# Token layers of a scan and attention hybrid: four images one behind the other in place of layer by layer, two of them beside the last outputs

## The chip, the cores and the metric

The kernel runs on one core of a Trainium2 chip. The metric is the device time in microseconds of one launch on that core. Before the change it is 10757.76 us, the median of 8 runs (10748.81 to 10774.99).

## The reference

The input is x, four images of 64 by 64 positions with 96 channels. Four layers follow, each added onto x:

```
x = x + conv_ref(group_norm(x), ...)          # layers 0 and 1: selective scan in four directions
t = tokens(x)                                 # (4, 4096, 96)
t = t + attn_ref(layer_norm(t), ...)          # layer 2, attention without softmax
t = t + ffn_ref(layer_norm(t), ...)           # layer 2, feed-forward in quantised floats
t = t + attn_ref(layer_norm(t), ...)          # layer 3
t = t + ffn_ref(layer_norm(t), ...)           # layer 3
```

The attention has no softmax: `y = (q @ k.T * D**-0.5) @ v` by head, so that k.T @ v can be formed first, from the Gram matrix of the normalised tokens. The feed-forward (96 to 384 to 96, relu between) rounds inputs and weights to a float of 5 exponent and 2 mantissa bits, and sums to half precision. All sums of an image's attention and all its norms need only that image: no layer mixes images. In a layer of selective scan, the output of an image is `layernorm(y) * silu(z)` times a matrix, added onto x.

## The kernel before, in words

The kernel is written for a scheduler that takes the instructions in the order of the program, places them on each engine's queue by priority of that order as soon as it reckons them ready, and gives out the buffers of a pool in the order in which the program asks for them. Tiles of one tag share that tag's buffers. Inside the scans (`scan_pair`, line 331) the class `InOrder` holds each engine to the program's order; their instructions are all recorded at line 71.

Four units of work come first: two scan layers, each in two pairs of images (lines 864 to 869). Before each unit `between_scans` (line 104) runs the outputs of the unit before (`scan_outputs`, line 247) beside the inputs of the next (`scan_inputs`, line 123), as two generators that are stepped in turn. After the fourth unit the outputs of images 2 and 3 of layer 1 run alone (line 869). `scan_outputs` goes over 16 groups of 256 positions. In each it loads zt, ys and xr, normalises ys (DVE statistics at 281, a power on POOL at 81, ACT at 289), transposes six blocks into the tile pt (296), scales them to gt on ACT (299), multiplies by zt on DVE (306), multiplies by the output matrix into po (310, 311), adds xr (313) and stores both images (316).

Then come the token layers. Each image is one tile tok of 128 partitions by 32 tokens by 96 channels, loaded at line 876. `attention` (718) runs for all four images, then `ffn` (774) for all four, then both again for layer 3 (lines 877 to 879). Each of the four calls opens pools of its own for weights, for work tiles and for PSUM, and closes them at its end; so their memory passes from one call to the next.

- `token_norm` (680): 32 statistics on DVE (684), six small steps on DVE, one power on POOL (81) for all 32 tokens of a partition, the shift (699), and 32 scalings into tn, 24 on ACT (705) and 8 on POOL (703).
- `attention`: 32 products on PE into gram (754), eight groups of four transposes into tnps with a copy to tnt on ACT (714, 715), four small products one after the other (739) with DVE between them, then eight groups of four products into ops (769) and a sum onto tok on DVE (771).
- `ffn`: eight transposed groups as above into xq (715), then eight chunks of 512 tokens. A chunk has three products into hps (809), each with a copy to h16 on ACT (811), bias and relu into hb16 on DVE (813) and a cast to hq on POOL (814); then twelve products into ops (818), a copy to o16 on ACT (822), a sum on DVE with the bias (824) and one onto tok (826). In layer 3 tok is then stored (828).

tn, tnt, xq, h16, hb16, hq, o16 and ob16 have two buffers each. In PSUM, hps of the feed-forward has three and tnps, ops, gram and small have two.

Of the kernel before, what the change touches and what calls it, by code (L numbers as in the profile page):

```python
# [16 lines left out]
F32 = mybir.dt.float32  # L17
BF16 = mybir.dt.bfloat16
F16 = mybir.dt.float16
E5M2 = mybir.dt.float8e5  # L20
AF = mybir.ActivationFunctionType
ALU = mybir.AluOpType
# [81 lines left out]
def between_scans(tc, cst, ident, half, u, before, after):  # L104


    with ExitStack() as stage:
        if before is None:
            for _ in scan_inputs(tc, stage, cst, ident, half, u, *after):
                pass  # L110
        elif after is None:
            for _ in scan_outputs(tc, stage, ident, half, *before):
                pass
        else:
            ins = scan_inputs(tc, stage, cst, ident, half, u, *after)
            for _ in scan_outputs(tc, stage, ident, half, *before):
                for _ in range(2):
                    next(ins, None)
            for _ in ins:
                pass  # L120
# [126 lines left out]
def scan_outputs(tc, stage, ident, half, layer, pr):  # L247
# [4 lines left out]
    pp = stage.enter_context(tc.tile_pool(name="c_ps", bufs=1, space=PSUM))  # L252
# [3 lines left out]
    for g in range(NT // 2):  # L256
# [36 lines left out]
        pt = pp.tile([128, 3, 2, 128], F32, name="pt")  # L293
        for j, first in enumerate((0, 256, 128)):
            for t in range(2):
                nc.tensor.transpose(pt[:, j, t], ys[:, t, first : first + 128], ident)
        gt = p2.tile([128, 3, 2, 128], F32, name="gt")
        for s, js in ((0, slice(0, 2)), (1, slice(2, 3))):
            nc.scalar.activation(
                gt[:, js],  # L300
                pt[:, js],
                AF.Identity,
                bias=par[:, s, P_NB : P_NB + 1],
                scale=par[:, s, P_NW : P_NW + 1],
            )
        nc.vector.tensor_tensor(gt, gt, zt.rearrange("p j (t q) -> p j t q", q=128), ALU.mult)
        po = pp.tile([128, 2, 2, C], F32, name="po")
# [372 lines left out]
def token_norm(nc, pool, half, t, tn):  # L680

    stats = pool.tile([128, NT, 6], F32, name="tstats")
    for j in range(NT):
        nc.vector.bn_stats(stats[:, j], t[:, j])  # L684

# [13 lines left out]
    nc.vector.scalar_tensor_tensor(shift, mean2, -0.5, rs, ALU.mult, ALU.mult)  # L699
    for j in range(NT):  # L700
        scale, bias = rs[:, j : j + 1], shift[:, j : j + 1]
        if j % 4 == 3:
            nc.gpsimd.tensor_scalar(tn[:, j, :C], t[:, j], scale, bias, ALU.mult, ALU.add)  # L703
        else:
            nc.scalar.activation(tn[:, j, :C], t[:, j], AF.Identity, bias=bias, scale=scale)  # L705


def turn_tokens(nc, pp, ident, tn, out):

    n = tn.shape[2]  # L710
    for g in range(NT // 4):
        ps = pp.tile([n, 512], F32, name="tnps", tag="tp")
        for j in range(4):
            nc.tensor.transpose(ps[:, 128 * j : 128 * j + 128], tn[:, 4 * g + j], ident)  # L714
        nc.scalar.activation(out[:, 512 * g : 512 * g + 512], ps, AF.Copy, saturate=False)


def attention(tc, cst, ident, half, tok, w):


    nc = tc.nc
    with ExitStack() as stage:
        p1 = stage.enter_context(tc.tile_pool(name="t1", bufs=1))
        p2 = stage.enter_context(tc.tile_pool(name="t2", bufs=2))
        pp = stage.enter_context(tc.tile_pool(name="t_ps", bufs=2, space=PSUM))

        wkv = p1.tile([C + 1, 2 * C], F32, name="wkv")
        nc.sync.dma_start(out=wkv, in_=w["wkv"])
        wq = p1.tile([C, C + 1], F32, name="wq")
        nc.sync.dma_start(out=wq, in_=w["wq"])  # L730
        wff = p1.tile([C, C], F32, name="wff")
        nc.sync.dma_start(out=wff, in_=w["Wff"])
        bff = p1.tile([C + 1, C], F32, name="bff")
        nc.sync.dma_start(out=bff, in_=w["bff"])

        def product(a, b, name):

            ps = pp.tile([a.shape[1], b.shape[1]], F32, name=name, tag="small")
            nc.tensor.matmul(ps, a, b, start=True, stop=True)
            return ps  # L740

        def kept(ps, name):
            to = p2.tile(list(ps.shape), F32, name=name)
            nc.vector.tensor_copy(to, ps)
            return to

        for b in range(NB):
            t = tok[b]
            tn = p2.tile([128, NT, C + 1], F32, name="tn")
            nc.gpsimd.memset(tn[:, :, C : C + 1], 1.0)  # L750
            token_norm(nc, p2, half, t, tn)
            gram = pp.tile([C + 1, C + 1], F32, name="gram")
            for j in range(NT):
                nc.tensor.matmul(gram, tn[:, j], tn[:, j], start=(j == 0), stop=(j == NT - 1))  # L754
            tnt = p2.tile([C + 1, L], F32, name="tnt")
            turn_tokens(nc, pp, ident, tn, tnt)
            gk = kept(product(kept(gram, "gram"), wkv[:, :C], "gkps"), "gk")
            vk = product(wkv[:, C:], gk, "vkps")

            heads = p2.tile([C, C], F32, name="heads")  # L760
            nc.vector.tensor_tensor(heads, cst["heads"], vk, ALU.mult)
            rest = kept(product(heads, wff, "hps"), "rest")
            whole = p2.tile([C + 1, C], F32, name="whole")
            nc.vector.tensor_tensor(whole, bff, product(wq, rest, "wps"), ALU.add)
            for g in range(NT // 4):
                po = pp.tile([128, 4, C], F32, name="ops", tag="o")
                for j in range(4):
                    at = 512 * g + 128 * j
                    nc.tensor.matmul(po[:, j], tnt[:, at : at + 128], whole, start=True, stop=True)  # L769
                tg = t[:, 4 * g : 4 * g + 4]  # L770
                nc.vector.tensor_tensor(tg, tg, po, ALU.add)


def ffn(tc, ident, half, tok, w, out=None):

    nc = tc.nc
    NH = HID // 128
    with ExitStack() as stage:
        p1 = stage.enter_context(tc.tile_pool(name="f1", bufs=1))
        p2 = stage.enter_context(tc.tile_pool(name="f2", bufs=2))  # L780
        pp = stage.enter_context(tc.tile_pool(name="f_ps", bufs=2, space=PSUM))

        def quantised(shape, src, name, back=False):
            raw = p1.tile(shape, F32, name=name)
            nc.sync.dma_start(out=raw, in_=src)
            q = p1.tile(shape, E5M2, name=name + "q")
            nc.vector.tensor_copy(q, raw, saturate=False)
            if back:
                nc.vector.tensor_copy(raw, q)
                return raw  # L790
            return q

        w1 = quantised([C, HID], w["W1"], "w1")
        w2 = quantised([128, NH, C], w["W2"].rearrange("(k p) c -> p k c", p=128), "w2")
        b1 = quantised([128, NH], w["b1"], "b1", back=True)
# [197 lines left out]
```

## Time and profile before

| what | us |
|---|---|
| median of 8 runs | 10757.76 |
| the profiled execution | 10772.43 |
| its span | 10770.6 |
| last outputs (10079 to 10204) | 125 |
| attention of layer 2 (10204 to 10335) | 131 |
| feed-forward of layer 2 (10335 to 10470) | 135 |
| attention of layer 3 (10470 to 10600) | 130 |
| feed-forward of layer 3 (10600 to 10771) | 171 |
| busy over the span: DVE, POOL, ACT, PE | 9622.8, 9028.6, 8755.0, 8109.2 |

The limits of the stages are those at which the work of one layer gives way to that of the next; neighbours overlap by a few us. PE is the time of matmuls, PEld that of weight loads, which lie beside them. DVE is VectorE, ACT ScalarE, POOL GpSimd, SP the queue from which transfers are issued. An instruction on SP counts only as issue, its transfer takes place later.

### The profile page before, as it was taken

The page shows a single profiled execution, that of the slowest core. Times are in us where ns is not written, and L with a number is a line of the kernel's source. Part 1 is how long each engine was busy: PE and PEld are TensorE (multiplying, and loading weights), DVE is VectorE, ACT ScalarE, POOL GpSimd, SP SyncE. Part 2 cuts the span into 40 slices and gives each one's busy share as a digit, 9 for nine tenths or more (in the row PEclk, how much of TensorE's full clock was granted, in tenths as well). Part 3 has the DMA queues.
Part 4 walks back from the last instruction along what each step waited for, and adds up shares of the span by engine and source line. Part 5 has one row for each costly group of instructions (what it writes and reads, how often), then busy time and mean ns, then how long its engine had stood idle before and what let it go on. Part 6 is the DMA issues. An engine that isn't in the chain of part 4 may idle for free. (4 is left out here: it accounts for less than half of the span.)

```text
span 10770.6 us, 143139 instructions
## 1 busy us (share of the span) xinstructions
PE 8109.2 (75%) x48032; PEld 6010.1 (56%) x48032; DVE 9622.8 (89%) x6898; ACT 8755.0 (81%) x18679; POOL 9028.6 (84%) x5306
## 2 busy tenths in 40 slices
PE   7777777777777777776877777777777777777666
PEld 4555555554555555555555555555455555555544
DVE  7999999997899999998899999999699999999655
ACT  6988888885898888886688888888588888888556
POOL 3999999992899999996599999999299999999444
PEclk9888898888888898998888888889888989898766
DMA  3677777775677777777577777777477777777600
GB/s 123 208 211 215 217 224 219 213 217 144 193 211 214 218 219 221 217 220 196 153 209 215 214 219 219 218 218 213 139 208 210 218 215 222 215 220 219 177 3 26
DMA packets 960473, 2114.17 MB, mean 196 GB/s; under 512 B 413526, under 2 KB 704664, under 8 KB 762008
## 3 DMA queue, kind: packets, MB, share of 16 engines
q1 hardware_dynamic: 959736, 2105.01, 68.0%
q8 instruction: 381, 6.24, 0.3%
q14 instruction: 356, 2.92, 0.1%
HBM read 1943.27 MB, written 161.48 MB: 195 GB/s over the span
## 5 line engine op out<-in xcount | busy, mean ns | idle before, releaser
L71 POOL TENSOR_TENSOR h<-h,cb 128x1024 f32<-128x1024 f32 x3072 | 7193.6, 2365 | 232.3 <-issue 57.9
L71 DVE TENSOR_TENSOR_SCAN h<-da,last,bp 128x1024 f32<-128x1024 f32 x2064 | 4736.7, 2335 | 144.8 <-PE bp L71 22.6
L71 ACT ACTIVATE x<-dut,bt 128x128 f32<-128x128 f32 x12288 | 3495.2, 370 | 1.3 <-PE bp L71 1.0
L71 PE MATMUL yp<-ident,h 128*128 128x128 f32 x24576 | 3352.9, 296 | 10.2 <-POOL h L71 10.2
L71 PEld LDWEIGHTS yp<-ident,h 128*128 128x128 f32 x24576 | 3179.4, 156 | 126.1 <-issue 75.1
L71 ACT ACTIVATE da<-delta,amat 128x1024 f32<-128x1024 f32 x2752 | 3060.7, 1138 | 96.9 <-DVE h L71 95.9
L71 PE MATMUL bp<-ident,x 128*128 128x128 f32 x10240 | 1674.5, 315 | 1293.4 <-DVE h L71 953.3
L71 PEld LDWEIGHTS bp<-ident,x 128*128 128x128 f32 x10240 | 1355.9, 162 | 1857.3 <-ACT x L71 1024.5
L71 DVE TENSOR_TENSOR bp<-du,bp 128x1024 f32<-128x1024 f32 x1472 | 1779.9, 1213 | 301.9 <-PE bp L71 300.1
L71 DVE TENSOR_TENSOR_SCAN h<-da,bp 128x1024 f32<-128x1024 f32 x688 | 1537.5, 2274 | 48.0 <-ACT da L71 8.5
L71 PE MATMUL bp<-bparts,sel 96*128 96x512 bf16 x2944 | 924.0, 399 | 756.9 <-DVE h L71 741.8
L71 PEld LDWEIGHTS <-sel 96*128 96x128 bf16 x2944 | 227.0, 100 | 1552.3 <-DVE h L71 1040.9
L71 ACT ACTIVATE bp<-delta,amat 128x1024 f32<-128x1024 f32 x320 | 358.4, 1120 | 525.7 <-DVE h L71 524.0
L71 POOL TENSOR_TENSOR dbu<-du,bb 128x1024 f32<-128x1024 f32 x320 | 755.1, 2360 | 0.0
L81 POOL TENSOR_TENSOR ln_rs<-ln_ve,half 128x4 f32<-128x4 f32 x64 | 83.9, 1311 | 593.4 <-DVE ln_ve L79 492.2
L71 DVE TENSOR_TENSOR_SCAN h<-bp,last,dbu 128x1024 f32<-128x1024 f32 x240 | 558.9, 2329 | 16.3 <-POOL dbu L71 15.1
L71 PE MATMUL xps<-u,wx 128*76 128x512 f32 x768 | 559.9, 818 | 5.7 <-ACT cdt L71 2.9
L71 POOL TENSOR_TENSOR du<-delta,u 128x1024 f32<-128x1024 f32 x192 | 506.6, 2638 | 21.7 <-ACT delta L71 21.7
L71 POOL COPY last<-h 128x2 f32<-128x2 f32 x1152 | 216.1, 188 | 341.4 <-DVE h L71 340.5
L71 ACT ACT_TABLE_LOAD x384 | 492.7, 1283 | 6.8
L71 PE MATMUL dps<-cdt,wdt 12*128 12x512 f32 x768 | 448.0, 665 | 0.0
L71 ACT COPY dut<-dups 128x512 f32<-128x512 f32 x384 | 220.7, 575 | 257.7 <-PE dups L71 257.7
(132 smaller groups left out, 6384.0 us busy)
## 6 DMA issues: line engine op xcount, KB each, us to landing
cb<-crow SPq DMA_DIRECT2D x1024, 1024.0 KB
cb<-crow SPq DMA_DIRECT2D x1024, 512.0 KB
bb<-crow SPq DMA_DIRECT2D x384, 256.0 KB
bb<-crow SPq DMA_DIRECT2D x128, 512.0 KB
y<-ysum SPq DMA_DIRECT2D x192, 256.0 KB
kept<-y SPq DMA_DIRECT2D x160, 256.0 KB
y<-ysum SPq DMA_DIRECT2D x64, 512.0 KB
zt<-zg SPq DMA_DIRECT2D x64, 384.0 KB
```

The costliest lines, as they stand in the source:

```text
L71: return self.tc.keep_in_program_order(getattr(self.engine, op)(*args, **kwargs))
L81: nc.gpsimd.tensor_tensor(rs, ve, half, ALU.pow)
```

## The change

The token layers become one function, `token_layers`, in which every image is a generator that runs attention and feed-forward of layer 2 and then of layer 3, and yields between small pieces: every 8 statistics, after the scale, every 8 scalings, every group of transposes, every group of attention sums, and twice in each chunk of the feed-forward. A layer pair of one image is some 51 such pieces. The loop steps the last scan outputs by one group and every image that has begun by one piece in each turn. Image b begins no earlier than turn 13 b; images 0 and 1 may begin while the outputs of images 2 and 3 still run, images 2 and 3 only once they are done, when their tok is loaded.

For that, all weights of both layer pairs are loaded at the start, and all token work shares one set of pools. The scan's large tiles are in pools that close before the token layers open theirs. tn has three buffers. hps goes from three PSUM buffers to two, gram and small from two to one. The last outputs use the PSUM tags of the token layers ("mm" for the transposes, "o" for the sums). In all four output stages the tile pt, six blocks in one buffer of two banks, becomes three blocks for each half of the tokens, in two buffers of one bank, and the two scalings on ACT become four.

```diff
-        pt = pp.tile([128, 3, 2, 128], F32, name="pt")
-        for j, first in enumerate((0, 256, 128)):
-            for t in range(2):
-                nc.tensor.transpose(pt[:, j, t], ys[:, t, first : first + 128], ident)
         gt = p2.tile([128, 3, 2, 128], F32, name="gt")
-        for s, js in ((0, slice(0, 2)), (1, slice(2, 3))):
-            nc.scalar.activation(
-                gt[:, js],
-                pt[:, js],
...
+        for t in range(2):
+            pt = pp.tile([128, 3, 128], F32, name="pt", tag=turned)
+            for j, first in enumerate((0, 256, 128)):
+                nc.tensor.transpose(pt[:, j], ys[:, t, first : first + 128], ident)
+            for s, js in ((0, slice(0, 2)), (1, slice(2, 3))):
+                nc.scalar.activation(
+                    gt[:, js, t],
+                    pt[:, js],
...
-        po = pp.tile([128, 2, 2, C], F32, name="po")
+        po = pp.tile([128, 2, 2, C], F32, name="po", tag=summed, bufs=1 if summed == "po" else None)
...
-    for n in (2, 3):
-        attention(tc, cst, ident, half, tok, {k: a[f"l{n}_{k}"] for k in ("wq", "wkv", "Wff", "bff")})
-        ffn(tc, ident, half, tok, {k: a[f"l{n}_{k}"] for k in ("W1", "b1", "W2", "b2")}, a["out"] if n == 3 else None)
+def token_layers(tc, cst, ident, half, x, outputs, a):
...
+        load(0)
+        load(1)
+        wa = [weights(attention_weights, n, ("wq", "wkv", "Wff", "bff")) for n in (2, 3)]
+        wf = [weights(ffn_weights, n, ("W1", "b1", "W2", "b2")) for n in (2, 3)]
...
+        def image(b):
+            for n in range(2):
+                yield from attend(n, b)
+                yield from feed(n, b)
+
+        outs = scan_outputs(tc, stage, ident, half, *outputs, pp, "mm", "o")
+        images = [image(b) for b in range(NB)]
+        begun, going, turns = 0, [], 0
+        while outs is not None or going or begun < NB:
+            if outs is not None and next(outs, outs) is outs:
+                outs = None
+                load(2)
+                load(3)
+            if begun < NB and turns >= 13 * begun and (begun < 2 or outs is None):
+                going.append(images[begun])
+                begun += 1
+            going = [one for one in going if next(one, going) is not going]
+            turns += 1
```

In the changed kernel `token_norm`, `attention` and `ffn` are generators over one image, with the same instructions in the same order within an image; `turn_tokens` makes one group of four transposes a call, so that in `attention` the eight groups stand between the gram products.

## The prediction

> **What bounds the kernel now.** I read first the page's row of busy tenths over the span (in its last slices DVE falls from 9 to 6 and 5, ACT to 5 and 6, POOL to 4), then busy time by stretch, then the groups of instructions by shape, the waits, and the order of time where they pointed. The change leaves the scans as they are, so the tail counts: the last outputs (10079 to 10204), attention of layer 2, feed-forward of layer 2, attention and feed-forward of layer 3. Columns: stretch, length, then busy us of PE, PEld, DVE, ACT, POOL, granted clock, DMA share, GB/s.
>
> ```profile
> 10079.00:10204.00 125.00, 74.15 (x352) 62.18 (x352) 52.42 (x192) 49.39 (x96) 16.10 (x16) 0.66 0.60 166
> 10204.00:10335.00 131.00, 85.75 (x680) 82.61 (x680) 60.79 (x297) 59.83 (x151) 46.37 (x50) 0.75 0.10 39
> 10335.00:10470.00 135.00, 86.03 (x532) 49.47 (x532) 83.30 (x210) 100.03 (x218) 84.82 (x110) 0.63 0.00 1
> 10470.00:10600.00 130.00, 93.11 (x741) 86.06 (x740) 67.82 (x280) 60.13 (x145) 45.55 (x54) 0.76 0.02 5
> 10600.00:10771.00 171.00, 99.18 (x608) 54.99 (x608) 103.66 (x276) 116.38 (x256) 106.56 (x132) 0.61 0.09 38
> 10204.00:10771.00 567.00, 364.08 (x2560) 273.13 (x2560) 315.57 (x1060) 336.36 (x768) 283.30 (x344) 0.68 0.06 22
> ```
>
> No engine is full. In the last row four engines do 364 + 316 + 336 + 283 = 1299 us of work in 567: 2.29 engines at a time. Attention has its own shape (PE ahead), feed-forward another (ACT ahead), and they stand one after the other for all four images. The waits of the tail say why:
>
> ```profile
> POOL tn_rs L81 <- DVE tn_ve L79: 158.4, 14, 47.9
> ...
> DVE tshift L699 <- POOL tn_rs L81: 90.7, 16, 8.7
> ...
> ACT tn L705 <- DVE tshift L699: 81.7, 8, 21.2
> ```
>
> ACT stands 82 us before norms whose scale isn't there. At the first one (order of time) statistics start at 10204.6, the 5.4 us power on POOL follows, and ACT starts at 10217.2. What can be reached is seen inside a feed-forward, chunk after chunk:
>
> ```profile
> 10646.79 0.54 DVE L826 TENSOR_TENSOR tok<-tok,ob 128x384 f32<-128x384 f32 x1
> 10647.26 0.96 DVE L813 TENSOR_SCALAR hb<-h,b 128x512 f16<-128x512 f16 x2
> 10648.31 0.78 DVE L824 TENSOR_TENSOR ob<-o,b 128x384 f16<-128x384 f16 x1
> 10649.01 0.70 DVE L813 TENSOR_SCALAR hb<-h,b 128x512 f16<-128x512 f16 x1
> 10649.63 0.54 DVE L826 TENSOR_TENSOR tok<-tok,ob 128x384 f32<-128x384 f32 x1
> ```
>
> A chunk takes 10649.63 - 10646.79 = 2.84 us with DVE nearly full. In 10640 to 10656 the engines were busy 12.24 + 14.71 + 11.72 + 12.60 = 51.3 us in 16: 3.2 at a time, the best that the tail shows. Without norms 32 chunks would take 91 us; the two feed-forwards took 135 and 171.
>
> **The Trainium skill.** "Perfetto Trace Analysis", Optimization Strategy: where the busiest engine changes from regime to regime, interleaving the regimes may help as well as work inside each. The first table agrees that it changes. "TensorE: Matmul & The Clock Gate", What's actually happening: idleness halves TensorE's clock, sustained work releases it. The trace agrees: sixteen products of L769 took 3.41 us at 10529.6 and 1.79 at 10552.6. "GPSIMD Engine Reference", Specifications: POOL shares its SBUF interface with VectorE. The cast of L814 is spread from 602 to 957 ns (median 804), which fits and doesn't prove it. "PSUM — Partial Sum Buffer", Specifications: eight banks of 2 KiB a partition; no run here shows it, and I use it for the count below.
>
> **The change part by part.**
>
> *Start.* The loads of images 0 and 1 and 16 weight loads now stand on SP ahead of the loads of the last outputs. In the built order (the order in which the changed program queues its instructions on each engine) the image loads come before the last store of the scan's sum (10074.6), the weights after it. The image loads wait for memory of the scan's inputs, whose last readers on PE and DVE end at about 10062 to 10069; behind them on SP stands that store alone, which is not ready before 10074.6, so this wait costs nothing. If their 3 MB were still moving when the outputs' first loads come, those loads would land later; that is in the upper bound. SP issues of such weights took 0.28 to 0.94 us at 10055 to 10058; 16 x 0.5 = 8 us. They push wo, zt and ys, which all outputs wait for, by about 8 us. On DVE the 64 statistics of images 0 and 1 stand ahead of the first ystats: 64 x 0.17 us (33 took 5.52) = 11 us, mostly inside that delay. I take 10 us, bounds 4 and 16.
>
> *Outputs.* 125 us for 16 groups is 7.8 us a group: po on PE (3.6 us), rest of pt (1.3), gt on ACT (1.2), gt by zt on DVE (1.0). pt is split by token half into two PSUM banks (1536 B each, before 3072 B in one two-bank buffer). By shape gt took 778 + 557 = 1335 ns. Two halves of 128x256 (557) and 128x128 (estimate 447, by the slope of the two) are 2008: ACT gains 0.67 x 16 = 11 us in each output stage. In the three stages between scans ACT is busy 109 of 227 us against PE 181, so that is hidden; the second pt buffer could give a little. I take 0, bounds -8 and +8 each, in sum -15 to +15 as they needn't add up. In the last outputs the split lets gt of one half start early, and norms of images put ACT work between; I keep 125 us, bounds 105 and 145.
>
> *What runs beside the outputs.* By the built order only normalisation, gram, transposes and the small products of images 0 and 1: their attention sums share tag "o" with the sixteen po and come after the last. Moved, a quarter or an eighth of each group: ACT tn 145.0/8 + tnt 35.7/4 = 27; DVE stats 91.0/8, small steps 2.7, products 2.5 = 17; POOL power 86.8/8 and tn 52.5/8 = 18; PE gram 63.4/4, transposes 40.3/4, products 3 = 29. Together 90 us of engine work, so half an attention of two images and not more.
>
> *After the outputs.* 1299 - 90 = 1209 us of work remain, with attention of one image beside feed-forward of another (built order: "0: xq, 2: tnt, 0: h ..." on ACT). Layer barriers, weight waits and three of four ramps go. Norms of one image should lie beside chunks of another. At 2.9 engines at a time that is 417 us. I chose 2.9 between 2.29 (today's mean) and 3.2 (best stretch), nearer the best, because norm gaps get a cover but queues in fixed order and two buffers each of h16, hb16, hq stay. Check on ACT: 336 - 27 = 309 us; at the start it must wait for the sums, statistics and power (some 25 us), at the end image 3 is nearly alone (10): 309/(417 - 35) = 81%, against 74% in the first feed-forward. hps goes from three buffers to two, gram and small from two to one (2+2+2+1+1 = 8 banks): PE needs 0.5 us for hps, ACT 0.59, so two suffice; 0, bound +5. The last store (6 us) stays.
>
> *Sum.* Outputs start at 10079 + 10, end at 10214, the rest ends at 10631: 10771 - 10631 = 140 us gone of the profiled execution, which took 10772.43 (span 10770.6 and 1.8 around it). That run is 14.7 us over the median, 10757.8; the saving taken off the median gives 10618.
>
> **Rivals.**
> 1. *Queues mesh better (10564).* At 3.2 engines throughout the rest takes 1209/3.2 = 378 us, and the outputs are 15 us shorter as PE warms up: 140 + 39 + 15 = 194 us saved. For it: no engine passes 364 us of 567. Against: DVE is already 92% full in that stretch.
> 2. *Fixed order eats it (10705).* At 2.4 the rest takes 504 us, 53 saved: DVE's queue mixes statistics of one image between hb and ob of another, and each wait holds all behind it. The wait ACT tn <- DVE tshift would stay near 80 us.
> 3. *Slower (10788).* One chunk in flight at a time: tag slots and DVE's order join the images. Unpipelined a chunk is transposes 0.9, xq 0.6, hps 0.5, h 0.6, hb 0.6, three hq 2.3, ops 1.4, o 0.5, ob 0.7, tok 0.6 = 8.7 us; 64 of them 557, with 35 for the ramps 592, ending at 10806: 35 us slower, less 5 of chunks that do overlap. It decides from 8.1 us a chunk ((557 - 35)/64). Against: 2.84 today.
> 4. *It doesn't do what it says:* half true above, since the attention sums can't pass the outputs; counted in the sum.
>
> **How the numbers follow.** Forecast (95 to 178 us saved) 0.48; rival 1 (more) 0.25; rival 2 (22 to 95) 0.21; rival 3 0.04; within 0.2% 0.02, a bound that is about what a measurement of this kernel can tell from no change. The likeliest is 10618. From 10550 (rival 1 and between-stage gain 15) to 10695 (2.45 at a time, 63 saved) I leave out some 7% below and 13% above. Faster 0.48 + 0.25 + 0.21 = 0.94.
>
> **What would show it.** First ystats about 10095; last xo about 10214; no gram work of images 2 and 3 before it; four engines' work in the rest near 1209 us in about 417; ACT tn <- tshift well under 82 us; the 64 casts o about (417 - 35)/64 = 6 us apart on the mean. Wrong if the outputs pass 150 us, if granted clock stays at 0.6 while PE becomes the last wait, or if ACT's 25 us start gap recurs at each layer.

## The result and the profile after

The changed kernel takes 10719.68 us, the median of 10 runs (10708.31 to 10730.28), the kernel before beside it 10762.04 (28 runs): a ratio of 0.9961, 95% interval 0.9953 to 0.9969. It is faster by 42 us, where 140 were predicted, and 10719.68 lies outside the range of 10550 to 10695. The profiled execution has a span of 10717.9 us, against 10770.6 before, so the two traces differ by 53 us, 10 more than the medians do.

The start of the tail wanders from profile to profile with the scans ahead of it, which no kernel here changes: over all twenty profiles the scan's last copy to ysum on ACT starts between 10060.5 and 10108.3 us. I therefore measure the tail from that copy (10073.6 before, 10075.5 after). The tail was 697.0 us and is 642.4: 55 us less. Busy time by stretch of the changed kernel (columns as in the prediction; the count of instructions is in brackets): up to the first ystats, to the last xo, to the first copy h of a feed-forward chunk, to the end.

```profile
10075.50:10107.70 32.20, 4.21 (x26) 4.21 (x27) 12.31 (x78) 5.73 (x15) 9.46 (x12) 0.52 0.72 215
10107.70:10224.50 116.80, 84.00 (x539) 73.61 (x537) 55.21 (x214) 77.04 (x180) 25.32 (x25) 0.79 0.50 136
10224.50:10277.80 53.30, 34.99 (x178) 32.59 (x178) 28.09 (x145) 18.37 (x50) 17.42 (x19) 0.56 0.17 64
10277.80:10717.90 440.10, 290.33 (x2175) 216.99 (x2174) 257.07 (x816) 286.84 (x654) 244.09 (x304) 0.79 0.04 15
```

The first ystats comes 32.2 us after the scan's last copy (11.3 before); the outputs then take 116.8 us (116.1 before). What follows the last xo is 53.3 + 440.1 = 493.4 us (569.6 before). In it PE, DVE, ACT and POOL do 325 + 285 + 305 + 262 = 1177 us of work: 2.39 engines at a time. Even the long last stretch, past the start gap, has only (290 + 257 + 287 + 244)/440 = 2.45. Before, it was 2.28 of 1300 us. So some 120 us of work are gone from the stretch after the outputs, most of it done beside them, and the concurrency has hardly moved.

The waits after the last xo (who waited, for whom, us in total, times, longest), one line of before first, then those of after:

```profile
POOL hq L814 <- DVE hb L813: 86.2, 128, 12.5
```

```profile
POOL hq L810 <- DVE hb L809: 165.6, 132, 12.0
PEld L814 <- POOL hq L810: 161.1, 123, 12.2
...
DVE tshift L696 <- POOL tn_rs L81: 74.4, 14, 8.2
...
ACT tn L703 <- DVE tshift L696: 53.5, 5, 33.8
```

ACT's wait for the scale (82 us before) went down to 53.5, of which 33.8 is one gap at the start. POOL's wait for hb, on the other hand, has risen from 86 to 166 us: POOL is idle for hb while PE is idle for POOL's hq. POOL in order of time shows what stands between them:

```profile
10353.86 0.88 POOL L810 CAST hq<-hb 128x512 fp8e5<-128x512 f16 x1 [0.37 <-DVE hb L809]
10354.92 5.44 POOL L81 TENSOR_TENSOR tn_rs<-tn_ve,half 128x32 f32<-128x32 f32 x1 [0.19 <-ACT tnt L714]
10360.69 4.11 POOL L701 TENSOR_SCALAR tn<-tok,tn_rs,tshift 128x96 f32<-128x96 f32 x8 [0.33 <-DVE tshift L696]
10364.76 1.16 POOL L810 CAST hq<-hb 128x512 fp8e5<-128x512 f16 x2
```

From 10354.92 to 10364.76 POOL casts no hq for any image: the power of one image's norm, then its eight scalings. In the same stretch DVE stands 5.30 us before the shift of that norm, until 10360.39, with an hb behind it whose h was there from 10355.35. A power of this length comes in each of the sixteen norms, fourteen of them after the last xo. The chain of waits from 10226 to the end names the power first:

```profile
by line: POOL tn_rs L81 14.6%; ACT tn L703 12.4%; PE ops L763 9.3%; DVE hb L809 8.9%; POOL tn L701 7.6%; POOL hq L810 7.1%; issue 6.3%; PE ops L814 5.4%; DVE tstats L679 4.7%; PE gram L747 3.6%; ACT h L807 2.6%; PE tnps L713 2.3%; DVE tok L
```

14.6% of 492 us is 72 us. (The line ends where the view cuts it.)

### The profile page after: what moved, and what is told of

It is laid out like the page before. It is cut to its first block, busy times and chain, and to the rows that moved or that the text cites. A ratio compares the mean times of both kernels' runs of the same rounds, so it can differ in the third digit from the quotient of the medians.

```text
span 10717.9 us, 143300 instructions
## 1 busy us (share of the span) xinstructions
PE 8097.7 (76%) x48032; PEld 6013.9 (56%) x48032; DVE 9607.5 (90%) x6898; ACT 8779.8 (82%) x18807; POOL 9030.2 (84%) x5306
## 4 chain that ended last, share of the span: by engine, by line
ACT 35%; PE 18%; DVE 17%; issue 17%; POOL 10%; DMA 2%; SPq 0%; DVEq 0%; POOLq 0%; ACTq 0%
ACT x L71 15%; ACT da L71 13%; DVE h L71 9%; PE yp L71 6%; POOL h L71 6%; PE bp L71 5%; DVE bp L71 4%; ACT bp L71 2%; DVE u L166 2%; PE xps L71 2%; DMA cb<-crow 1%; PE dps L71 1%; ACT L71 1%; PE dups L71 1%; POOL dbu L71 1%
## 5 line engine op out<-in xcount | busy, mean ns | idle before, releaser
L71 DVE TENSOR_TENSOR_SCAN h<-bp,last,dbu 128x1024 f32<-128x1024 f32 x240 | 558.9, 2329 | 10.8 <-POOL dbu L71 7.9
L71 ACT COPY ysum<-yp 128x1024 f32<-128x1024 f32 x192 | 194.4, 1013 | 290.9 <-PE yp L71 290.9
```

The source lines that it names most:

```text
L71: return self.tc.keep_in_program_order(getattr(self.engine, op)(*args, **kwargs))
```

## The experiments

All runs were timed against the kernel before on the same chip. The first column is the ratio to it, with its interval; the other columns are from the profiles. "Start" is from the scan's last copy to the first ystats, "outputs" from there to the last xo, "rest" from there to the end, "work" the busy time of PE, DVE, ACT and POOL in the rest. A profiled run lies up to 18 us from its kernel's median, and 29 in k1, so the last four columns tell where the time lies in that run and the ratio what a kernel is worth.

| kernel | median us | ratio (95%) | start | outputs | rest | work / rest |
|---|---|---|---|---|---|---|
| before | 10762.04 | 1 | 11.3 | 116.1 | 569.6 | 2.28 |
| changed | 10719.68 | 0.9961 (0.9953 to 0.9969) | 32.2 | 116.8 | 493.4 | 2.39 |
| f1, loads after outputs | 10714.65 | 0.9952 (0.9940 to 0.9965) | 15.7 | 117.9 | 492.9 | 2.39 |
| g1, nothing beside outputs | 10746.85 | 0.9982 (0.9976 to 0.9989) | 19.5 | 116.8 | 527.1 | 2.38 |
| f2, layer by layer | 10735.02 | 0.9969 (0.9957 to 0.9980) | 32.0 | 119.0 | 502.2 | 2.42 |
| f4, chunk in two pieces | 10715.86 | 0.9955 (0.9942 to 0.9969) | 31.8 | 119.4 | 486.8 | 2.42 |
| f5, shorter runs of scalings | 10735.08 | 0.9972 (0.9962 to 0.9982) | 32.1 | 114.6 | 510.7 | 2.32 |
| h2, power in four pieces | 10735.65 | 0.9965 (0.9952 to 0.9977) | 33.0 | 119.5 | 500.1 | 2.40 |
| h3, root, and a spare power | 10693.20 | 0.9928 (0.9916 to 0.9940) | 26.6 | 113.3 | 479.2 | 2.47 |
| p1, root on ScalarE | 10642.24 | 0.9887 (0.9873 to 0.9900) | 26.6 | 109.0 | 423.9 | 2.59 |
| h1, before with root | 10693.32 | 0.9925 (0.9912 to 0.9937) | 11.2 | 116.3 | 490.7 | 2.45 |
| h4, layer by layer with root | 10628.06 | 0.9870 (0.9855 to 0.9885) | 27.4 | 106.5 | 419.5 | 2.63 |
| k1, layer by layer, nothing beside outputs | 10738.31 | 0.9972 (0.9962 to 0.9982) | 19.1 | 114.8 | 523.5 | 2.45 |
| p2, root and early outputs | 10635.35 | 0.9881 (0.9868 to 0.9895) | 15.9 | 110.7 | 421.5 | 2.61 |
| p3, as p2, chunk in two pieces | 10617.44 | 0.9863 (0.9848 to 0.9878) | 15.3 | 110.4 | 411.4 | 2.67 |
| k2, layer by layer, root, early outputs, buffers | 10617.47 | 0.9856 (0.9841 to 0.9871) | 15.7 | 111.9 | 418.9 | 2.61 |

Ratios are to the kernel before on the same chip at the same time, whose median went from 10762 to 10773 us, so differences between kernels are taken from the ratios: 0.001 is 10.8 us, and by the intervals a difference of two ratios is known to some 0.0014 to 0.002.

**First four: three theories of the shortfall.** Theory A: DVE's queue is held by the shift, which waits for the power. Theory B: two buffers are too few. Theory C: each of several queues has a fixed order and no single one is the cause.

The shift moved to POOL, behind the power:

```diff
+    nc.vector.tensor_scalar(mean2, mean2, -0.5, None, ALU.mult)
     rs = rstd_of(nc, pool, var, [128, NT], "tn", half)
     shift = small("tshift")
-    nc.vector.scalar_tensor_tensor(shift, mean2, -0.5, rs, ALU.mult, ALU.mult)
+    nc.gpsimd.tensor_tensor(shift, mean2, rs, ALU.mult)
```

> The shift of a token norm is worked out on POOL, right behind the power that it needs, in place of DVE; DVE has one small step more ahead of the power. In the changed kernel DVE stood 85 us before the sixteen tshift, with all its later work queued behind. Theory A (DVE's queue is held by the power's wait, and the chunks of other images with it): 10650 to 10680, 40 to 70 us under the changed kernel's 10720, and the wait of DVE for the power near 0. Theory B (two buffers each of h16, hb16, hq hold the chunks): under 10 us, 10710 or more. Theory C (several queues' order together, none alone): 10 to 35 us, the stall moves on to ACT's scalings standing ahead of h.

Measured: 10722.35 us, ratio 0.9954 (0.9941 to 0.9966), as the changed kernel. Its waits in the rest:

```profile
POOL hq L811 <- DVE hb L810: 175.7, 130, 14.6
...
ACT tn L704 <- POOL tshift L697: 74.7, 9, 34.7
...
DVE hb L810 <- POOL hq L811: 55.1, 15, 14.6
```

DVE no longer waits for the power, but ACT waits longer for the shift (75 us against 53.5), and DVE now stands 55 us before buffers of hb that POOL has not read. Theory A falls: with DVE freed, the time stays and POOL is still late.

Four buffers for h16, hb16 and hq, three for o16, ob16 and xq:

```diff
-            h = pool.tile([128, 512], F16, name="h16")
+            h = pool.tile([128, 512], F16, name="h16", bufs=4)
```

> h16, hb16 and hq have four buffers, o16, ob16 and xq three, in place of two; PSUM as in the changed kernel. Theory B: 40 us or more under 10720, and POOL's wait for hb (165 us) falls by half. Theories A and C: within 10 us of 10720, since the chunk's pieces stand in the queues behind other images' work and not before a full buffer.

Measured: 10726.95 us, ratio 0.9959 (0.9946 to 0.9971). POOL's wait for hb is 175.9 us. Theory B falls.

Three groups of the outputs issued ahead of the loads of images 0 and 1 and of the weights:

```diff
+        outs = scan_outputs(tc, stage, ident, half, *outputs, pp, "mm", "o")
+        for _ in range(3):
+            next(outs)
         load(0)
         load(1)
```

> The first three groups of the last outputs are issued ahead of the loads of images 0 and 1 and of the 16 weight loads. In the changed kernel the first ystats came at 10107.7, against 10084.9 before. If the weight loads on SP are what held the outputs, first ystats comes back to about 10087, the last xo from 10224.5 to about 10205, and the time falls by 12 to 20 us (10700 to 10708). Rival: the images' first work comes later by as much and nothing is gained, 10715 to 10725.

Measured: 10720.05 us, ratio 0.9954 (0.9940 to 0.9967). The first ystats came 15.8 us after the scan's last copy in place of 32.2, but the last xo 146.2 in place of 149.0: the later groups' loads then stood behind the weights. Nothing gained.

Images begun by the loop only once the outputs are through:

```diff
-            if begun < NB and turns >= 13 * begun and (begun < 2 or outs is None):
+            if begun < NB and turns >= 16 + 13 * begun and outs is None:
```

> All four images begin only once the last outputs are done; their weights and the tiles of images 0 and 1 are still loaded first. It shows what the part beside the outputs is worth. Theory (90 us of engine work is hidden there, which at some 2.4 engines at a time is 37 us): 10745 to 10765, 25 to 45 us over the changed kernel. Rival (what runs beside the outputs is paid back in the 52 us after them in which no chunk runs): within 10 us of 10720.

Measured: 10722.18 us, ratio 0.9953 (0.9940 to 0.9965); but the trace has the same tail as the changed kernel (642.1 us), with gram of images 0 and 1 beside the outputs. The scheduler had put work that was ready ahead of later outputs whatever the loop said. The run tells nothing of the overlap.

**What the work beside the outputs is worth.** First all outputs issued ahead of all loads; then also a dependency from the outputs to the loads:

```diff
+        outs = scan_outputs(tc, stage, ident, half, *outputs, pp, "mm", "o")
+        for _ in outs:
+            pass
+        for b in range(NB):
+            load(b)
```

> All four token images are loaded, and so begun, only after the last outputs have been issued; nothing of them can run beside the outputs. In the earlier run that only moved the step that begins them, the scheduler still put the first norms ahead of the outputs, so it priced nothing. If the work of images 0 and 1 beside the outputs is worth what it is worth elsewhere in the tail (about 88 us of engine work at 2.39 engines at a time is 37 us, less the 13 us by which the outputs then start earlier): about 24 us slower than the changed kernel, 10740 to 10755. If the work beside the outputs is given back later (the first image waits at its power and the others behind it anyway): 10715 to 10727.

```diff
         nc.vector.tensor_tensor(xo, xr, po, ALU.add)
+        for late in gone or ():
+            nc.vector.tensor_copy(late[:, 0, :2], xo[:, 0, 0, :2])
```

> The loads of all four images now wait for the last outputs themselves (a two-element copy from each group's xo into the tokens of images 0 and 1, overwritten by the load), since with the loads only issued later the scheduler still let them and the first norms run beside the outputs. Nothing of the images lies beside the outputs; the load of image 0, some 10 us, is bare. If the work beside the outputs is worth what it is worth elsewhere (88 us of engine work at 2.39 engines at a time, 37 us, less 16 us of earlier outputs, plus 10 us of load): about 30 us slower than the changed kernel, 10745 to 10760. If it is worth nothing since the stretch after the outputs is set by a chain through the images and not by the amount of work: within 8 us of the changed kernel, 10712 to 10728.

In the first, the images' norms still ran beside the outputs, since nothing but the place in the program held them. It gives another number: the outputs start after 15.7 us, end 15.4 us earlier after the scan, and the rest takes the same time, 492.9 us. The tail is 626.5 us, 16 less than in the changed kernel; of that the ratios show 10 us (0.9952 against 0.9961), with intervals that overlap. In the second nothing of the images is there before 10227.3 (their first statistics, last xo 10218.9):

```profile
10218.90:10746.00 527.10, 342.43 (x2560) 266.60 (x2560) 300.81 (x1051) 331.19 (x768) 278.93 (x341) 0.77 0.06 25
```

The rest grows by 33.7 us, of which 8.4 are the bare load; its work by 1253 - 1177 = 76 us. With the earlier outputs the tail is 21 us longer, and by the ratios (0.9982 against 0.9961) the kernel 23 us slower. So the overlap is real: in this order 76 us of work lie beside the outputs and save some 25 us after them; the load order that goes with it costs up to 16 us of late outputs.

**Is it the interleaving?** Layer by layer, image after image, in the one set of pools and with weights early:

```diff
+        def layers():
+            for n in range(2):
+                for make in (attend, feed):
+                    for b in range(NB):
+                        yield from make(n, b)
+
+        rest = layers()
+        for _ in outs:
+            next(rest)
```

> All weights early, one set of pools, the first attention layer begun beside the outputs, but the images no longer interleaved by hand: the pieces are issued layer by layer and image after image, as before the change. Theory C (the interleaving gains little since every engine takes its queue in a fixed order, and the 42 us come from the removed boundaries and from the work beside the outputs): 10705 to 10735, the same as the changed kernel. Rival (the interleaving is what gained, the boundaries cost little): 10745 to 10762, near the kernel before.

```profile
10231.90:10734.10 502.20, 347.72 (x2353) 270.32 (x2351) 296.05 (x961) 307.98 (x704) 262.00 (x322) 0.71 0.05 20
```

10735.02 us, ratio 0.9969: 33 us of gain without any interleaving by hand. The interval (0.9957 to 0.9980) overlaps with that of the changed kernel; what the interleaving adds is 9 us by the ratios, by the traces the 9 us between rests of 502.2 and 493.4, and the medians can't tell it from nothing.

> Each feed-forward chunk is cut into two pieces, the first product with its three casts, and the second product with what follows, so that a piece of every other image lies between them; h16, hb16 and hq have four buffers, o16, ob16 and xq three; the images follow each other at 15 pieces instead of 13. Theory D (TensorE stands at the second product until the chunk's own chain product, h, hb, hq has run, since nothing else is put between: 161 us of its weight loads waited for hq): 15 to 45 us faster than the changed kernel, 10675 to 10705. Theory C in the form that ScalarE's runs of token scalings hold the casts: no more than 8 us either way, 10710 to 10728.

A yield was put between the casts to hq and the second product, images 15 turns apart, with the buffers above. 10715.86 us: no gain that can be told from none, and less than theory D asked for. But the wait that the split was to take away hardly moved: PE's loads still waited 151.3 us for hq, against 161.1. The run shows that this split doesn't shorten the wait, and leaves open what a chunk's own chain costs.

> The token norm yields after every four tokens' statistics and scalings instead of every eight, with the images 17 pieces apart instead of 13: on ScalarE's queue the runs of scalings ahead of the casts of h and o shrink from up to 12 to up to 6. Theory C in the form that these runs hold the chunks of the other images: 10 to 30 us faster, 10690 to 10710. Theory D (a chunk's own chain is what is waited for): within 6 us, 10714 to 10726.

Yields after every four tokens, images 17 turns apart. 10735.08 us, by the ratios 12 us slower than the changed kernel (the intervals just overlap), outside both expectations. The edit did what it was meant to: in the rest, ACT's runs of more than six scalings fell from sixteen to three. In the changed kernel twelve scalings do stand ahead of casts of h, as at 10384, where two products hps were there from 10386.51:

```profile
10384.57 4.40 ACT L703 ACTIVATE tn<-tok,tshift,tn_rs 128x96 f32<-128x96 f32 x12
...
10385.45 1.06 PE L805 MATMUL hps<-xq,w1q 96*128 96x512 fp8e5 x2
...
10388.87 1.06 ACT L807 CAST h<-hps 128x512 f16<-128x512 f32 x2
...
10390.30 1.17 POOL L810 CAST hq<-hb 128x512 fp8e5<-128x512 f16 x2 [10.82 <-DVE hb L809]
```

But shortening such runs bought nothing. They are easily seen in the trace, and yet not the cause.

**The power.** What remained was the first line of the chain, the 5.4 us power:

```diff
-    rs = rstd_of(nc, pool, var, [128, NT], "tn", half)
+    ve = small("tn_ve")
+    nc.vector.tensor_scalar(ve, var, EPS, None, ALU.add)
+    rs = small("tn_rs")
+    nc.scalar.activation(ve, ve, AF.Sqrt)
+    nc.vector.reciprocal(rs, ve)
```

> The token norm's power on GpSimd (5.43 us for 128x32, sixteen of them) is replaced by a square root on ScalarE and a reciprocal on VectorE; nothing else is changed. Theory E (the powers are the thread of the tail: they take 14.6% of the chain of waits after the outputs, 72 of 492 us, since hq of the other images stands behind each on GpSimd and the image's own scalings wait for it): 13 powers on the chain by about 4.2 us saved is 55 us, and with a second chain close behind 20 to 55 us faster than the changed kernel, 10665 to 10700. Theory C (whichever single wait is taken away, the next engine in the fixed order takes its place, as when the shift was moved and when buffers were added): 10710 to 10728.

10642.24 us, ratio 0.9887 against 0.9961: 80 us faster than the changed kernel, more than the theory asked for. The root takes 0.23 us and the reciprocal 0.34 us, with one table load of 1.28 us on ACT. The rest falls from 493.4 to 423.9 us:

```profile
10215.00:10638.90 423.90, 322.15 (x2352) 248.27 (x2351) 286.09 (x975) 306.02 (x718) 183.53 (x309) 0.81 0.06 24
```

PE, DVE and ACT do the same work as in the changed kernel; POOL has 78 us less, and the rest is 69 us shorter. How it acted was open: by filling POOL's queue, or by making the image itself wait for its power. A spare power, computed on POOL into a tile that nobody reads beside the root that is used, keeps POOL's queue full and frees the image itself:

```diff
+    spare = small("spare")
+    nc.gpsimd.tensor_tensor(spare, ve, half, ALU.pow)
+    root = small("root")
+    nc.scalar.activation(root, ve, AF.Sqrt)
+    nc.vector.reciprocal(rs, root)
```

> The root on ScalarE and VectorE as in the run with it alone (10642 us), and the old power still computed on GpSimd into a tile that nobody reads: GpSimd's queue as in the changed kernel, the image's own wait gone. Occupancy: most of the 77 us come back, 10700 to 10725. Latency: 10640 to 10665.

```profile
L698 POOL TENSOR_TENSOR spare<-tn_ve,half x16: 5421/5436/5477, 10101.1 to 10642.0; 128x32 f32<-128x32 f32 x16
```

```profile
10219.20:10698.40 479.20, 333.82 (x2352) 260.00 (x2351) 286.66 (x975) 307.29 (x718) 256.18 (x323) 0.76 0.05 21
```

10693.20 us, ratio 0.9928: an operation for which nobody waits brings back 0.0041, 44 of the 80 us (in the rest 55 of 69), each known to some 20 us. The spare power doesn't act by slowing VectorE, whose busy time in the rest is 286.7 us with it and 286.1 without. The time lies between the two expectations: about half of the cost or more is POOL's queue. The remainder is put down to the image's own wait by subtraction alone. Now the same power in four pieces, the scalings after each:

```diff
+    for q in range(4):
+        at = slice(8 * q, 8 * q + 8)
+        nc.gpsimd.tensor_tensor(rs[:, at], ve[:, at], half[:, at], ALU.pow)
+        nc.vector.scalar_tensor_tensor(shift[:, at], mean2[:, at], -0.5, rs[:, at], ALU.mult, ALU.mult)
...
+        yield
```

> The changed kernel with the power in four pieces of 128x8 (about 1.6 us each by the 1.0 us of 128x4 and the 5.4 us of 128x32), each followed by its shift and its eight scalings, with a yield after it: GpSimd is as busy as before or a little more, but the image's scalings start after the first piece and other images' casts can stand between the pieces. Latency (an image waits for its own whole power) or long blocks ahead of other casts: 25 to 60 us faster than the changed kernel, 10660 to 10695. Occupancy (87 us of power on GpSimd's queue have to be done in any case): 10705 to 10730.

```profile
L701 POOL TENSOR_TENSOR tn_rs<-tn_ve,half x64: 1628/1637/2042, 10107.7 to 10684.9; 128x8 f32<-128x8 f32 x64
```

64 x 1.637 = 104.8 us of power against 16 x 5.435 = 87.0: 18 us more on POOL, and a ratio of 0.9965, not faster than the changed kernel's 0.9961. Shorter blocks and an earlier first scaling, 25 us and more by the first expectation, bought nothing or were eaten by the 18 us. That fits occupancy, as the spare power does.

**Is the power why the interleaving fell short?** The same root in the kernel before and in the layer-by-layer order:

> The kernel before the change, with the token norm's power replaced by the square root on ScalarE and the reciprocal on VectorE. Theory E2 (the power costs most in the interleaved order, where the other images' casts stand behind it on GpSimd; in the kernel before, the powers take 6.8% of the chain of 562 us after its outputs, 38 us): 15 to 40 us faster than before, 10725 to 10752, so that the change is worth 85 to 110 us once the power is gone. Rival (the power costs as much in either order, and the interleaving itself is worth only the 42 us): 70 to 85 us faster, 10680 to 10697.

> The layer-by-layer order (10735 us with the power) with the root on ScalarE. If the power hid what the interleaving is worth: interleaved and not differ by 40 to 70 us now, 10682 to 10712, where they differed by 15. If the power costs as much in either order: 10650 to 10665, again about 15 us behind.

Before with root: 10693.32 us, ratio 0.9925, a gain of 81 us, as the rival had it (the rest went from 569.6 to 490.7 us, the work in it from 2.28 to 2.45 engines at a time); the 38 us in the chain of before were no bound on what the power cost there. Theory E2 falls. With the root on both sides the change is worth 0.9925 - 0.9887 = 0.0038 of the time, 41 us (known to some 20), as it is worth 42 without. So the power made both kernels slower and is not why the change gained less than was forecast. And layer by layer with the root is 10628.06 us, faster than both expectations for it and no slower than the interleaved order with it (0.9870 and 0.9887, intervals overlap). There the root gained 0.0099, 107 us; that this is more than the 80 in the interleaved order can't be told from scatter. Its rest:

```profile
10208.20:10627.70 419.50, 308.05 (x2352) 228.66 (x2351) 297.40 (x975) 309.72 (x718) 186.42 (x308) 0.77 0.06 24
```

2.63 engines at a time without interleaving by hand, 2.59 with it. In neither pair, with the power or without, does the interleaving raise the concurrency.

**What gives the 42 us.** Layer by layer with nothing beside the outputs, by the same dependency as above:

> Layer by layer in one set of pools, and all images' loads wait for the last outputs, so that neither the interleaving nor the work beside the outputs is there: what is left of the change is the removed boundaries between layers and the weights loaded early. If the three parts add (interleaving 15 us, work beside the outputs 27 us, boundaries the rest): 10755 to 10768, no gain to speak of over the kernel before. If the boundaries and weights are the main gain: 10715 to 10745.

10738.31 us, ratio 0.9972 (0.9962 to 0.9982), nine runs from 10727 to 10767: by the ratio 30 us faster than the kernel before, as the second expectation had it. Its profiled run was the slowest of the nine, but what made it slow lies ahead of the tail: its second and third scans took 2308 us each, against 2288 to 2296 in all other profiles. Measured from the scan's end, the tail is 657.4 us, 40 less than before and 15 more than in the changed kernel. The parts don't add: taking away the work beside the outputs costs the interleaved order 23 us, the layer-by-layer order 3 by the ratios, with intervals 0.002 wide. What stands is that what is left of the change gives some 30 of the 42 us alone, and that the interleaving by hand is not needed for it. What is left is more than one set of pools and early weights: tn has a third buffer, pt is split, and the order within an image isn't the same in one respect. In the program of the kernel before all eight groups of transposes of a feed-forward stand ahead of its chunks, in the changed one each group just ahead of its chunk, and in attention between the gram products. Which of these gives the 30 us was not tried apart. The early weights are an unlikely source: in the trace before, all waits for weights after the outputs sum to 1.0 us.

**A version that beats both.**

> The root on ScalarE together with the outputs issued ahead of all images and weights (which by itself brought the outputs forward by 16 us in the trace of the run with the images loaded after them). Theory E: both add up, 10650 to 10690. Theory C: only the 16 us at most, 10702 to 10720.

> As the run before, and the feed-forward chunk in two pieces with four buffers. With the power gone GpSimd no longer holds the casts of hq for 5 us at a time, so what is left of the chunk's own chain should count more. If the chunk's chain is then what is waited for: 10 to 30 us faster than the run with the root and the early outputs. If not: within 8 us of it.

> Layer by layer with the root on ScalarE (10628 us), the outputs issued ahead of all images and weights, and four buffers for h16, hb16 and hq, three for o16, ob16 and xq. If the early outputs give the 7 us that they gave the interleaved order with the root, and the buffers let the casts of several chunks of a layer run ahead: 10600 to 10622, the best of all. If the layer-by-layer order already begins as much as its buffers allow: 10622 to 10635.

Root and early outputs: 10635.35 us, below both expectations as the root alone was, and by the ratios (0.9881 and 0.9887) not told apart from it. With the chunk in two pieces and the buffers: 10617.44, all four runs below all four of the one before; by the ratios 19 us, as expected. Layer by layer with root, early outputs and buffers: 10617.47, in the first expectation, though the 15 us to layer by layer with the root alone (0.9856 and 0.9870) can't be told from none. The last two are the best and can't be told apart: 1.4% below the kernel before, 1% below the changed one, and one of the two has no interleaving by hand.

So there are four pairs of kernels that are the same or nearly the same but for the interleaving (interleaved first, ratios): changed and f2, 0.9961 and 0.9969; g1 and k1, 0.9982 and 0.9972; p1 and h4, 0.9887 and 0.9870; p3 and k2, 0.9863 and 0.9856. Every pair's intervals overlap, and the interleaved kernel is the faster only in the first.

## Why the prediction was wrong, by its steps

- *Start, +10 us (bounds 4 and 16): too small.* The first ystats came 21 us later against the scan's end (32.2 against 11.3). The issues of the weights on SP took longer than those that the trace before showed (rows: start, duration):

```profile
10079.76 1.55 SPq L721 DMA_DIRECT2D wkv<-in_l_wkv  x1
...
10083.56 2.48 SPq L721 DMA_DIRECT2D wkv<-in_l_wkv  x1
...
10088.79 3.42 SPq L774 DMA_DIRECT2D w<-in_l_W  x2
...
10095.27 0.38 SPq L249 DMA_DIRECT2D wo<-in_l_wo  x1
```

  16 issues last 15.5 us until wo follows, not 16 x 0.5 = 8. With the outputs first, 16.5 of the 21 us were gone (15.7): the weight loads on SP are the cause. This is 10.5 us of the miss: the last xo is at 10224.5, not 10214.
- *Outputs unchanged in length: right,* 116.8 against 116.1 us by the first ystats and the last xo. The half of gt by 128x128 took 451 ns (estimate 447).
- *Between stages 0: inside the bounds, perhaps a small loss.* From the last scan instruction of a unit to the first of the next, the three stages together took 721.9 us before and 718.4 in the kernel before with the root, 725.4 in the changed kernel and 722.6 to 729.4 in all profiles with the split pt. That is a loss of some 6 us if anything; the scatter of the tail's start comes from the scans.
- *Beside the outputs 90 us of work: nearly right,* 76 by the run with nothing there. No gram work of images 2 and 3 was there (128 of 512 products, two images).
- *After the outputs 1209 us of work: right,* 1177, though with a part that the prediction didn't have: hb, hq and ob took 298 us before and 264 after, for the same number of instructions.
- *"At 2.9 engines at a time that is 417 us": the step that failed.* It was 2.39 and 493.4 us: 76 of the 87 us by which the end was missed (10631 predicted, 10717.9 seen). I took 2.9 from between the mean of the tail and its best 16 us, and gave two reasons for going so near the best: one image's attention would lie beside another's feed-forward, and norms would lie beside chunks.

  The first reason failed. Layer by layer reaches the same concurrency in both pairs of runs (2.42 and 2.39; 2.63 and 2.59), and in none of the four pairs above is the interleaved kernel faster by more than the scatter, so the weaving by hand filled nothing that can be shown. The first table of the prediction, with PE ahead in one stage and ACT in the next, was true, and the Trainium skill ("Perfetto Trace Analysis", Optimization Strategy) says only that interleaving such regimes may help; here no run shows that it did.

  The second reason failed too. The best 16 us were chunks of one feed-forward with no norm in them, and norms are part of the rest: sixteen powers, 87 us in the tail, were counted as POOL work that can lie beside anything. The runs show that they can't: sixteen that nobody reads cost 44 us, and the powers in all 80. This held the level down in the kernel before as well (81 us), so it tells in part why 2.9 was out of reach, and not why the change gained only 42.

  The best stretch was also too high a mark in itself, which the trace before shows. Where hb on DVE lay for more than half of its time beside a cast to hq on POOL, it took 694 ns (median of 164), where no cast lay beside it 352 ns (24); hq took 804 ns beside hb (168) and 613 without (24). In the changed kernel they meet less often, and the medians of all 192 fall (least, median, most in ns):

```profile
L813 DVE TENSOR_SCALAR hb<-h,b x192: 335/679/698, 10350.5 to 10760.1; 128x512 f16<-128x512 f16 x192
L814 POOL CAST hq<-hb x192: 602/804/957, 10350.9 to 10760.9; 128x512 fp8e5<-128x512 f16 x192
```

```profile
L809 DVE TENSOR_SCALAR hb<-h,b x192: 327/354/804, 10278.4 to 10707.7; 128x512 f16<-128x512 f16 x192
L810 POOL CAST hq<-hb x192: 602/613/1038, 10278.9 to 10708.4; 128x512 fp8e5<-128x512 f16 x192
```

  So a part of the 3.2 engines at a time was two engines holding each other up. In those 16 us ten of fifteen hb took some 0.70 us and five 0.34. With every hb at 0.34 and every hq at 0.61 the stretch would hold 45 us of work and not 51, or 2.8 engines at a time (an estimate from these figures), less than the 2.9 that was asked of the whole rest.
- *Rival 2* had the time (10705) and, in broad words, the mechanism: a fixed order in which each wait holds what is behind it. Its place was wrong: it named DVE's queue, and relieving that alone changed nothing that can be told, while a power on POOL's queue for which nobody waits cost 44 us. Its sign, ACT's wait for the shift near 80 us, did not come (53.5).
- *Rival 3*, one chunk in flight, did not come: 64 copies of o in (10710.1 - 10282.3)/63 = 6.8 us steps, where it asked for 8.1 and more. The sign set for the forecast was 6.

What stays open: with the root, the rest is still at 2.6 engines at a time, with 162 us of waits of POOL for hb and 107 us of PE's loads for hq. Two pieces of a chunk, with more buffers, gave 18 us there and nothing to speak of with the power in place; what keeps it from 2.9 was not found. Nor were POOL's own scalings (4.11 us after the power in the stretch above) taken away.

## What to carry to other kernels

A best stretch is a fair level for a stage only if it holds every kind of work of that stage, and if its instructions take no longer there than they do alone: busy time counts the time in which two engines hold each other up as work. An operation of 5 us on an engine that also carries a step of every chunk has to be priced as a stop for all that is queued behind it. The test is to add a copy that nobody reads. Before weaving stages by hand, run the old order in the new pools: here it gave most of the gain, and the weaving nothing that could be told from zero. Check in the trace that an experiment moved what it meant to move: this scheduler pulled ready work ahead until a true dependency held it, and a split chunk left the wait it was aimed at where it was.

## What was not expected of the hardware

- The power on GpSimd is paid by the element: 1.01 us for 128x4, 1.64 for 128x8 and 5.43 for 128x32, 0.16 us for each further element of a partition. A root and a reciprocal of 128x32 take 0.23 us on ScalarE and 0.34 on VectorE.
- The same hb on VectorE took 352 ns where no cast to hq lay beside it on GpSimd and 694 ns where one did, and the cast 613 and 804 ns (medians, kernel before). That they meet in time is seen; no run took the one away to see the other.
- Issues of small weight loads on SP took from 0.28 us (bff) to 2.48 us (wkv), and the same wkv 1.55 us a few issues before, in a stretch in which the DMA share was 0.72. The trace doesn't show what held them.
- With the power gone from POOL the outputs became shorter as well, 109.0 us against 116.8, though the power that the outputs use themselves was left as it was; POOL did one whole power fewer in that stretch and one fewer just ahead of it. With the spare powers in their place the outputs took 113.3 us.
